# A two-layer graph kernel on one Trainium2 core: its gather ring in two pools, additions of beta pinned, ranks scattered in pairs

## The chip, the cores and the metric

The kernel runs on one core of one Trainium2 chip. A core has a matrix engine (TensorE, PE in the profile), a vector engine (VectorE, DVE), a scalar engine (ScalarE, ACT), a general engine (GpSimd, POOL) and one that only issues transfers (SyncE, SP). Each takes its own instructions in order and waits for others by semaphores. A name with a q (SPq, ACTq) is an engine's issuing side. The metric is device microseconds (us) of one execution, lower is better; three runs before the change gave a median of 2438.08.

## The reference, and what is computed

x has 8 batches of 2048 nodes with 256 features; adj is a sparse symmetric 2048x2048 matrix with a full diagonal. Two layers run one after the other, both over the same adj:

```python
# layer 0: attention, softmax within chunks of 256 columns, 4 heads
scores = clip(q @ k / 8, -10, 10); scores = where(mask == 0, -10, scores)
ctx = softmax_per_chunk(scores) @ v
out = ctx @ Wo.T + bo + x
out = (out - mean) * rsqrt(var + 1e-5) * gamma + beta
x = layernorm(x + out)
# layer 1: attention by e = s_src[j] + s_dst[i], leaky relu 0.2, masked softmax, then elu
x = layernorm(x + elu(alpha @ (x @ W)))
```

## The kernel before, in words

Everything is float32. The batches are taken in four pairs (g = 0 to 3, `G = 2`); the nodes in 16 blocks of 128 (`NT`). Since adj is sparse, each node gathers only its neighbours.

**Row lists** (`edge_lists`, lines 45 to 168). Sixteen steps load 128 rows of adj each (line 72, alternately on SP and ACT), mark the neighbours with their column number (line 74, with `jrow`, which comes from an iota on GpSimd, lines 57 to 59), count them on ACT (line 76) and take the largest 24 column numbers (lines 86 to 92). After each step one table step of pair 0 follows (`between`, line 96). Then each node gets its rank by number of neighbours: eight blocks on VectorE (line 106) and, beside them, eight on ACT (line 109), with a correction and a cast to integers for all (111, 113). GpSimd scatters the records of 16 blocks to DRAM in order of rank (line 117), SP loads them sorted (`srt`, line 120), and VectorE makes from them `node`, `nodeb`, `valid`, `idx` and the masks `same` (lines 124 to 148). After sorting, a block's row lists have a known longest length: `CAPS`, 24 slots for block 0 down to 5 for block 15, 164 in all.

**Tables** (`tables`, lines 351 to 409). For each pair and block: keys and values (`kv_d`) and queries with the residual (`qx_d`) are made on PE, copied by ACT and stored by SP. Every second step loads the next x (`load_x`, line 318) into one of two buffers `xt`, transposes it (line 334), and hands the previous `xt` to `add_beta` (line 344), which adds beta on GpSimd (line 348) and stores it (SP, line 349). The buffer is free for the next load after that store.

**Passes.** The main loop (lines 786 to 825) takes 64 steps of layer 0, order 15, 13, ... 1, 0, 2, ... 14 within a pass over one pair, and from the third pass on 32 steps of layer 1 between and after them. A step of layer 0 gathers by indirect transfer from GpSimd, a slot (one neighbour for 128 nodes) at a time (line 475, `fetch0`), multiplies with the query (VectorE, lines 533 and 540), sums by head on PE (552, 562), takes the softmax (line 573 on), weights the values (VectorE 487, ACT 493), sums them on PE (500) and copies the context out (ACT, line 612). `fetch` runs one step ahead. Pass g also makes the tables of pair g + 1, one block a step.

**Ring.** Gathered slots lie in 14 units of two slots each (`RING`, `UNIT`, lines 422 to 430), taken in turn. Each is zeroed once by VectorE, since a gather leaves slots without a neighbour as they were.

**What sets the order.** The kernel is written against a scheduler. It places the instructions of each engine by its own estimate of when they are ready, near the order of the source but not in it, and gives buffers from pools. When a pool is closed its memory goes to later pools, whose first use waits for the last use of the old tiles. So the pools of the preparation (`prep`, lines 234 to 293), of the lists (416) and of the ring (422) share memory in that order.

Of the kernel before, what the change touches and what calls it, by code (L numbers as in the profile page):

```python
# [9 lines left out]
F32 = mybir.dt.float32  # L10
BF16 = mybir.dt.bfloat16
I32 = mybir.dt.int32
I8 = mybir.dt.int8
AF = mybir.ActivationFunctionType
ALU = mybir.AluOpType
AX = mybir.AxisListType

P = 128
# [16 lines left out]
TOP = 24  # L35
REC = 32
G = 2
UNIT = 2
RING = 14
WW = 520  # L40
EMIN = 4.5399929762484854e-05

# [2 lines left out]
def edge_lists(tc: tile.TileContext, pool, bank, adj, const, ident, rec_d, B, between):  # L45
# [4 lines left out]
    nc = tc.nc  # L50
    N = adj.shape[0]
    NT = N // P
# [9 lines left out]
    rec = pool.tile([P, NT, REC], F32, name="rec")  # L62
# [5 lines left out]
    krow = pool.tile([P, N], F32, name="krow")  # L68

    for it in range(NT):  # L70
# [4 lines left out]
        junk = pool.tile([P, N], BF16, tag="junk", name="junk", bufs=1)  # L75
        nc.scalar.activation(junk, v, AF.Sign, accum_out=rec[:, it, TOP:TOP + 1])
        nc.vector.scalar_tensor_tensor(key[:, it:it + 1], rec[:, it, TOP:TOP + 1], float(N), nid[:, it:it + 1],
                                       op0=ALU.mult, op1=ALU.add)
# [9 lines left out]
        for r in range(TOP // 8):  # L88
            top = rec[:, it, r * 8:(r + 1) * 8]
            nc.vector.max(out=top, in_=cf)  # L90
            if r + 1 < TOP // 8:
# [3 lines left out]
                                accum_out=rec[:, it, TOP + 1:TOP + 2])  # L95
        between(it)


    rank = const.tile([P, NT], F32, name="rank")

    half = NT // 2
    nkey = pool.tile([P, NT], F32, name="nkey")
    nc.vector.tensor_scalar(nkey, key, -1.0, None, op0=ALU.mult)
    for it in range(half):
        gt = pool.tile([P, N], F32, tag="v", name="v", bufs=2)
        nc.vector.tensor_scalar(gt, krow, key[:, it:it + 1], 0.0, op0=ALU.is_gt, op1=ALU.add,
                                accum_out=rank[:, it:it + 1])
        junk = pool.tile([P, N], BF16, tag="junk", name="junk", bufs=1)
        nc.scalar.activation(junk, krow, AF.Sign, bias=nkey[:, half + it:half + it + 1],
                             accum_out=rank[:, half + it:half + it + 1])  # L110
    nc.vector.tensor_scalar(rank[:, half:], rank[:, half:], 0.5, 0.5 * (N - 1), op0=ALU.mult, op1=ALU.add)
    rank_i = pool.tile([P, NT], I32, name="rank_i")
    nc.vector.tensor_copy(rank_i, rank)

    views = dram_disjoint_views(rec_d, NT)
    for it in range(NT):
        nc.gpsimd.indirect_dma_start(out=views[it], out_offset=bass.IndirectOffsetOnAxis(ap=rank_i[:, it:it + 1], axis=0),
                                     in_=rec[:, it, :], in_offset=None)
    srt = pool.tile([P, NT, REC], F32, name="srt")
    nc.sync.dma_start(srt, rec_d.rearrange("(t p) r -> p t r", p=P))  # L120

    vals = srt[:, :, 0:TOP]
    node = const.tile([P, NT], I32, name="node")
    nc.vector.tensor_copy(node, srt[:, :, TOP + 2])
    nodeb = const.tile([P, NT, 2 * G], I32, name="nodeb")
    for b in range(2 * G):
        nc.vector.tensor_scalar(nodeb[:, :, b], srt[:, :, TOP + 2], float((B - 2 * G + b) * N), None, op0=ALU.add)
    valid = const.tile([P, NT, TOP], I8, name="valid")
    nc.vector.tensor_scalar(valid, vals, 0.0, None, op0=ALU.is_gt)
    far = pool.tile([P, NT, TOP], F32, name="far")  # L130
# [1 line left out]
    nc.vector.scalar_tensor_tensor(far, vals, -1.0, far, op0=ALU.add, op1=ALU.add)  # L132
    idx = const.tile([P, NT, TOP], I32, name="idx")
    nc.vector.tensor_copy(idx, far)

    chunk = pool.tile([P, NT, TOP], F32, name="chunk")
    nc.vector.tensor_scalar(chunk, vals, 0.0, None, op0=ALU.is_gt)
# [26 lines left out]
    op = bank("mf", 1)[0:1, 0:1]  # L164
# [7 lines left out]
def sparse_path(ctx: ExitStack, tc: tile.TileContext, keep, x, adj, Wq, bq, Wk, bk, Wv, bv, Wo, bo, gamma, beta, W, a,  # L172
                out):
    nc = tc.nc
    B, N, F = x.shape
    KC = F // P
    NT = N // P
# [6 lines left out]
    rec_d = nc.dram_tensor("rec_d", [N, REC], F32).ap()  # L184
# [5 lines left out]

    wh_d = [nc.dram_tensor(f"wh_d{p}", [N, 2 * WW], F32).ap() for p in range(NG // 2)]

# [4 lines left out]
    const = ctx.enter_context(tc.tile_pool(name="const", bufs=1))  # L197
# [8 lines left out]
    eps = const.tile([P, 1], F32, name="eps")  # L206
    nc.gpsimd.memset(eps, EPS)
    gamma_r = const.tile([P, F], F32, name="gamma_r")
    beta_r = const.tile([P, F], F32, name="beta_r")
# [24 lines left out]
    with tc.tile_pool(name="prep", bufs=2) as prep:  # L234
# [36 lines left out]
        for k, (v, scale) in enumerate(((bq, 0.125), (bk, 1.0))):  # L271
# [3 lines left out]
                                 scale=scale)  # L275
# [68 lines left out]
    def add_beta(g, t):  # L344

        xt = xTs.pop((g, t))[2]
        xv = xt.rearrange("p k (b f) -> p (k b) f", b=G)
        nc.gpsimd.tensor_tensor(xv, xv, beta_r.unsqueeze(1).to_broadcast([P, 2 * G, F]), op=ALU.add)  # L348
        nc.sync.dma_start(qx_d[g][t * P:(t + 2) * P, GF:].rearrange("(k p) f -> p k f", p=P), xt)

    def tables(g, t):
        if t % 2 == 0:
            if t:
                add_beta(g, t - 2)
            if g * NT + t + 2 < NG * NT:
                load_x(*divmod(g * NT + t + 2, NT))
            chunk_x(g, t)
        xT, xC, xt = xTs[g, t - t % 2]
        rows = slice(t % 2 * P, (t % 2 + 1) * P)
        if t == NT - 1:  # L360
            add_beta(g, t - 1)
# [49 lines left out]
    def first_tables(t):  # L411
        if t == 0:
            load_x(0, 0)
        tables(0, t)

    with tc.tile_pool(name="lists", bufs=1) as pool:
        with nc.allow_low_precision("exact small integers"):
            idx, valid, same, node, nodeb, rank, over = edge_lists(tc, pool, bank, adj, const, ident, rec_d, B,
                                                             first_tables)
        nc.vector.tensor_copy(keep, over)  # L420

    ring = ctx.enter_context(tc.tile_pool(name="ring", bufs=1))

    def unit():

        return ring.tile([P, UNIT, 2 * WW], F32, tag="u", name="u", bufs=RING)


    for _ in range(RING):
        nc.vector.memset(unit(), 0.0)  # L430
    sd = [const.tile([P, NT, 2, GH], F32, name=f"sd{p % 2}") for p in range(2)]

    def spread(src, sums, n):
# [35 lines left out]
    def gather(width, table, idx, t):  # L469
        units = []  # L470
        for s0 in range(0, CAPS[t], UNIT):
            u = unit()
            n = min(UNIT, CAPS[t] - s0)
            for k in range(n):
                nc.gpsimd.indirect_dma_start(  # L475
                    out=u[:, k, 0:width], out_offset=None, in_=table,
                    in_offset=bass.IndirectOffsetOnAxis(ap=idx[:, t, s0 + k:s0 + k + 1], axis=0),
                    bounds_check=N - 1, oob_is_err=False)
            units.append((u[:, 0:n], s0, n))
        return units  # L480
# [8 lines left out]
    def weighted_act(part, al, s0, n):  # L489
        for k in range(n):  # L490
            for e in range(part.shape[2] // D):
                pe = part[:, k, e * D:(e + 1) * D]
                nc.scalar.activation(pe, pe, AF.Copy, scale=al[:, e, s0 + k:s0 + k + 1])  # L493
# [23 lines left out]
    def scores0(g, t):  # L517
# [46 lines left out]
        for unit in units[npe:]:  # L564
            reduced(*unit)
# [73 lines left out]
    def rows1(g, t):  # L639
# [4 lines left out]
        nc.scalar.copy(xT, pt)  # L644
        wh = work.tile([P, WW], F32, tag="whs", name="whs")
        for b in range(G):
# [5 lines left out]
            nc.scalar.copy(wh[:, GF + b * H:GF + (b + 1) * H], pw[:, F + H:F + 2 * H])  # L652
        nc.sync.dma_start(wh_d[g // 2][t * P:(t + 1) * P, g % 2 * WW:(g % 2 + 1) * WW], wh)

# [3 lines left out]
    def fetch1(p, t):  # L658
        got1[p, t] = gather(2 * WW, wh_d[p], idx1, t)

# [28 lines left out]
    def context1(p, t):  # L689
# [5 lines left out]
        for i, (u, s0, n) in enumerate(units):  # L695
            for k in range(2):
                if i >= len(units) - na[k]:
                    weighted_act(u[:, :, k * WW:k * WW + GF], e[:, k * GH:(k + 1) * GH], s0, n)
        for i, (u, s0, n) in enumerate(units):
# [72 lines left out]
    def at(i):  # L772
        return i // NT, order[i % NT]
# [12 lines left out]
    for k, (layer, i) in enumerate(seq):  # L786
        g, t = at(i)
# [46 lines left out]
@with_exitstack  # L834
def kernel(ctx: ExitStack, tc: tile.TileContext, *args):
    nc = tc.nc
    flag = ctx.enter_context(tc.tile_pool(name="flag", bufs=1))
    over = flag.tile([1, 1], I32, name="over_keep")
    sparse_path(tc, over, *args)
    n_over = nc.values_load(over[0:1, 0:1], min_val=0, max_val=1 << 20)  # L840
    with tc.If(n_over > 0):
        dense_path(tc, *args)
# [417 lines left out]
```

## Time and profile before

| what | us |
|---|---|
| median of 3 runs (lowest, highest) | 2438.08 (2430.17, 2441.8) |
| the profiled execution | 2424.8 |
| its span on the core | 2423.1 |
| busy PE / DVE / ACT / POOL | 1885.1 / 1842.2 / 1401.9 / 1472.6 |
| copies of the context (line 612), step 0 / 15 / 16 / 31 | at 284.4 / 648.7 / 669.6 / 1033.2 |

Busy time is the sum of an engine's instructions within the span, so 1885.1 of 2423.1 means that PE was at work 78% of it, over stages with different limits. Times of instructions are counted from the start of the span. A line such as L348 is that of the kernel before, with the numbers printed above.

### The profile page before, as it was taken

What the parts mean: (1) busy time and instruction counts of PE and PEld (TensorE: products, weight loads), DVE (VectorE), ACT (ScalarE), POOL (GpSimd) and SP (SyncE); (2) the same over time, 40 slices, a digit from 0 to 9 for tenths busy, and PEclk for the clock granted to TensorE, in tenths of its full rate; (3) what the DMA queues carried; (4) which work ended last, traced back from release to release, by engine and by line L of the source; (5) the groups of instructions that cost most, each with busy time, mean ns of one, the idle gap of its engine ahead of it and who ended that gap; (6) DMA issues with size and microseconds to landing.
All of it is one profiled execution on the core that took longest, in us unless ns stands there. A gap on an engine that the chain in (4) does not pass through costs nothing. (4 is left out here: it accounts for less than half of the span.)

```text
span 2423.1 us, 38937 instructions
## 1 busy us (share of the span) xinstructions
PE 1885.1 (78%) x11946; PEld 1618.3 (67%) x11946; DVE 1842.2 (76%) x4095; ACT 1401.9 (58%) x5031; POOL 1472.6 (61%) x1225
## 2 busy tenths in 40 slices
PE   6786886689888889898899997776767775455764
PEld 5665675577777778777777776765666665445653
DVE  5975567878767888778889887887878886556775
ACT  4582354355555566555566675666346577556766
POOL 1123644686546667366678657775778754767874
PEclk9998898899989999999999998897888987777877
DMA  6745877598879679598879979896679975986873
GB/s 221 278 172 159 314 266 249 209 337 320 291 261 319 249 267 388 180 375 316 300 267 351 346 247 360 306 308 216 220 254 334 360 256 185 386 279 231 282 277 111
DMA packets 240750, 669.11 MB, mean 276 GB/s; under 512 B 44455, under 2 KB 70826, under 8 KB 238486
## 3 DMA queue, kind: packets, MB, share of 16 engines
q0 software_dynamic: 156800, 505.01, 59.1%
q1 hardware_dynamic: 80016, 151.56, 17.0%
q10 hardware_dynamic: 3718, 9.97, 1.2%
q8 instruction: 98, 1.61, 0.3%
q14 instruction: 118, 0.97, 0.1%
HBM read 612.79 MB, written 126.36 MB: 305 GB/s over the span
## 5 line engine op out<-in xcount | busy, mean ns | idle before, releaser
L475 POOL DMA_INDIRECT u<-kv_d,idx x656 | 802.2, 1223 | 423.0 <-PE acc L500 159.2
L500 PE MATMUL acc<-ident,u 128*128 128x128 f32 x5248 | 727.7, 295 | 191.6 <-DVE u L487 118.4
L500 PEld LDWEIGHTS acc<-ident,u 128*128 128x128 f32 x5248 | 649.9, 153 | 254.8 <-DVE u L487 166.1
L475 POOL DMA_INDIRECT u<-wh_d,idx x328 | 398.5, 1215 | 158.7 <-issue 68.9
L552 PE MATMUL pr<-ident,u 128*128 128x128 f32 (+1 forms) x1984 | 280.5, 291 | 78.5 <-DVE u L533 62.4
L487 DVE TENSOR_TENSOR u<-u,al 128x1024 f32<-128x1024 f32 x280 | 331.2, 1216 | 1.3
L533 DVE TENSOR_TENSOR u<-u,qx 128x1024 f32<-128x1024 f32 (+1 forms) x248 | 296.4, 1195 | 32.1 <-DMA u<-kv_d,idx 25.7
L487 DVE TENSOR_TENSOR u<-u,z 128x1024 f32<-128x1024 f32 x266 | 315.0, 1213 | 0.8
L552 PEld LDWEIGHTS pr<-ident,u 128*128 128x128 f32 (+1 forms) x1984 | 240.9, 148 | 108.0 <-DVE u L533 85.7
L493 ACT ACTIVATE u<-u,z 128x64 f32<-128x64 f32 x1008 | 261.0, 336 | 27.2 <-DVE z L686 27.2
L493 ACT ACTIVATE u<-u,al 128x64 f32<-128x64 f32 x800 | 210.7, 342 | 39.0 <-DVE al L593 38.4
L348 POOL TENSOR_TENSOR xt<-xt,beta_r 128x1024 f32<-128x1024 f32 x32 | 78.6, 2462 | 177.9 <-PE tk L334 151.6
L382 PE MATMUL tk<-wq,xT 128*128 128x256 f32 x512 | 149.6, 408 | 37.3 <-ACT kvs L376 37.3
L649 PE MATMUL mf<-wa,x1T 128*128 128x264 f32 x512 | 158.5, 435 | 21.0 <-ACT x1T L644 10.9
L369 PE MATMUL tk<-wkv,xT 128*128 128x256 f32 x512 | 144.9, 396 | 14.7 <-ACT xC L339 14.5
L621 PE MATMUL mf<-wo,cT 128*128 128x256 f32 x512 | 144.8, 406 | 10.6 <-ACT whs L652 9.9
L373 PE MATMUL tk<-wkv,xC 128*128 128x256 f32 x512 | 144.4, 398 | 0.0
L540 DVE TENSOR_TENSOR u<-u,qx 128x1024 f32<-128x1024 f32 (+1 forms) x96 | 110.3, 1152 | 44.6 <-DMA qx<-qx_d,node 23.9
L649 PEld LDWEIGHTS mf<-wa,x1T 128*128 128x128 f32 x512 | 97.4, 208 | 55.3 <-ACT whs L652 23.3
L441 ACT ACTIVATE sq<-o,nm 128x256 bf16<-128x256 f32 x256 | 129.4, 506 | 5.0
L382 PEld LDWEIGHTS tk<-wq,xT 128*128 128x128 f32 x512 | 94.4, 204 | 51.0 <-ACT kvs L376 42.0
L437 ACT ACTIVATE nm<-sums 128x2 f32<-128x2 f32 (+1 forms) x160 | 32.4, 202 | 160.0 <-DVE sums L627 82.0
(166 smaller groups left out, 3164.9 us busy)
## 6 DMA issues: line engine op xcount, KB each, us to landing
kv_d<-kvs SPq DMA_DIRECT2D x48, 512.0 KB
wh_d<-whs SPq DMA_DIRECT2D x64, 260.0 KB
xt<-in_x_dram SPq DMA_DIRECT2D x64, 256.0 KB
qx_d<-xt SPq DMA_DIRECT2D x32, 512.0 KB
qx_d<-qs SPq DMA_DIRECT2D x64, 256.0 KB
x_d<-o SPq DMA_DIRECT2D x64, 256.0 KB
xr<-x_d SPq DMA_DIRECT2D x32, 512.0 KB
u<-kv_d,idx POOLq DMA_INDIRECT x656, 6.5
```

Source lines behind the costliest of these rows:

```text
L369: nc.tensor.matmul(pm[:, 0:F], xT[:, b * KC + kc, rows], wkv[:, kc, 0:F], start=(kc == 0), stop=False, skip_group_check=True)
L373: nc.tensor.matmul(pm[:, F:], xC[:, b * KC + kc, rows], wkv[:, kc, F:], start=False, stop=(kc == KC - 1), skip_group_check=True)
L382: nc.tensor.matmul(qb, xT[:, b * KC + kc, rows], wq[:, kc, :], start=(b == 0 and kc == 0), stop=False, skip_group_check=True)
L441: nc.scalar.activation(sq, src[:, k, :], AF.Square, bias=nm[:, k:k + 1], accum_out=m2[:, k:k + 1])
L475: nc.gpsimd.indirect_dma_start(out=u[:, k, 0:width], out_offset=None, in_=table, in_offset=bass.IndirectOffsetOnAxis(ap=idx[:, t, s0 + k:s ...
L487: nc.vector.tensor_tensor(pv, pv, av, op=ALU.mult)
L493: nc.scalar.activation(pe, pe, AF.Copy, scale=al[:, e, s0 + k:s0 + k + 1])
L500: nc.tensor.matmul(acc[:, c, :], part[:, k, c * P:(c + 1) * P], ident, is_transpose=True, start=first and k == 0 and c == 0, stop=last and ...
L533: nc.vector.tensor_tensor(prod.rearrange("p k j (s w) -> p k j s w", w=W8), u[:, :, 0:GF].rearrange("p s (k j w) -> p k j s w", k=UNIT, w=W8),
L552: nc.tensor.matmul(pr[0:n * W8, k, :], prod[:, j // (NJ // UNIT), j % (NJ // UNIT), :], ident, is_transpose=True, start=(j == 0), stop=(j ...
L621: nc.tensor.matmul(po[:, b, :], cT[:, b * KC + kc, :], wo[:, kc, :], start=(b == 0 and kc == 0), stop=False, skip_group_check=True)
L649: nc.tensor.matmul(pw[:, 0:F + 2 * H], xT[:, b * KC + kc, :], wa[:, kc, :], start=(kc == 0), stop=(kc == KC - 1))
```

## The change

Five edits, all but one in the part before the first gather:

- The ring has two pools. `ring0` has five units (`RING0`) and is opened ahead of the lists' pool, so that it takes memory beside the lists; `ring1` has nine and is opened after it. Units are still taken in turn, 14 in all.
- The five units of `ring0` are zeroed by GpSimd ahead of the lists; of the nine of `ring1`, five are zeroed by ACT (a copy with scale 0) and four by VectorE.
- The addition of beta is held in the order of the source (`keep_in_program_order`) for all 32 of its calls.
- Ranks are corrected and cast pair by pair, block `it` with block 8 + `it`, and each pair of blocks is scattered at once; before, all sixteen followed the last rank.
- `nodeb`, which only the last scatters use, stands after `idx` in the source.

```diff
+RING0 = 5
@@ edge_lists
+    views = dram_disjoint_views(rec_d, NT)
     for it in range(half):
         gt = pool.tile([P, N], F32, tag="v", name="v", bufs=2)
         nc.vector.tensor_scalar(gt, krow, key[:, it:it + 1], 0.0, op0=ALU.is_gt, op1=ALU.add,
                                 accum_out=rank[:, it:it + 1])
         junk = pool.tile([P, N], BF16, tag="junk", name="junk", bufs=1)
-        nc.scalar.activation(junk, krow, AF.Sign, bias=nkey[:, half + it:half + it + 1],
-                             accum_out=rank[:, half + it:half + it + 1])
-    nc.vector.tensor_scalar(rank[:, half:], rank[:, half:], 0.5, 0.5 * (N - 1), op0=ALU.mult, op1=ALU.add)
-    rank_i = pool.tile([P, NT], I32, name="rank_i")
-    nc.vector.tensor_copy(rank_i, rank)
-
-    views = dram_disjoint_views(rec_d, NT)
-    for it in range(NT):
-        nc.gpsimd.indirect_dma_start(out=views[it], out_offset=bass.IndirectOffsetOnAxis(ap=rank_i[:, it:it + 1], axis=0),
-                                     in_=rec[:, it, :], in_offset=None)
+        k = half + it
+        nc.scalar.activation(junk, krow, AF.Sign, bias=nkey[:, k:k + 1], accum_out=rank[:, k:k + 1])
+        nc.vector.tensor_scalar(rank[:, k:k + 1], rank[:, k:k + 1], 0.5, 0.5 * (N - 1), op0=ALU.mult, op1=ALU.add)
+        nc.vector.tensor_copy(rank_i.rearrange("p (h t) -> p t h", h=2)[:, it], rank.rearrange("p (h t) -> p t h", h=2)[:, it])
+        for k in (it, half + it):
+            nc.gpsimd.indirect_dma_start(out=views[k],
+                                         out_offset=bass.IndirectOffsetOnAxis(ap=rank_i[:, k:k + 1], axis=0),
+                                         in_=rec[:, k, :], in_offset=None)
...
-    nodeb = const.tile([P, NT, 2 * G], I32, name="nodeb")
-    for b in range(2 * G):
-        nc.vector.tensor_scalar(nodeb[:, :, b], srt[:, :, TOP + 2], float((B - 2 * G + b) * N), None, op0=ALU.add)
...
     nc.vector.tensor_copy(idx, far)
+    nodeb = const.tile([P, NT, 2 * G], I32, name="nodeb")
+    for b in range(2 * G):
+        nc.vector.tensor_scalar(nodeb[:, :, b], srt[:, :, TOP + 2], float((B - 2 * G + b) * N), None, op0=ALU.add)
@@ add_beta
-        nc.gpsimd.tensor_tensor(xv, xv, beta_r.unsqueeze(1).to_broadcast([P, 2 * G, F]), op=ALU.add)
+        tc.keep_in_program_order(
+            nc.gpsimd.tensor_tensor(xv, xv, beta_r.unsqueeze(1).to_broadcast([P, 2 * G, F]), op=ALU.add))
@@ ahead of the lists' pool
+    rings, turn = [ctx.enter_context(tc.tile_pool(name="ring0", bufs=1))], [0]
+
+    def unit():
+
+        k = int(turn[0] % RING >= RING0)
+        turn[0] += 1
+        return rings[k].tile([P, UNIT, 2 * WW], F32, tag="u", name="u", bufs=RING - RING0 if k else RING0)
+
+    for _ in range(RING0):
+        nc.gpsimd.memset(unit(), 0.0)
+
@@ after it
-    ring = ctx.enter_context(tc.tile_pool(name="ring", bufs=1))
-
-    def unit():
-
-        return ring.tile([P, UNIT, 2 * WW], F32, tag="u", name="u", bufs=RING)
-
-    for _ in range(RING):
-        nc.vector.memset(unit(), 0.0)
+    rings.append(ctx.enter_context(tc.tile_pool(name="ring1", bufs=1)))
+    for n in range(RING0, RING):
+        u = unit().rearrange("p s w -> p (s w)")
+        if n % 2:
+            nc.scalar.activation(u, eps.to_broadcast([P, UNIT * 2 * WW]), AF.Copy, scale=0.0)
+        else:
+            nc.vector.memset(u, 0.0)
```

More of the change, by code (lines that the diff above doesn't have):

```diff
@@ L99, in edge_lists @@
     rank = const.tile([P, NT], F32, name="rank")
+    rank_i = pool.tile([P, NT], I32, name="rank_i")
     half = NT // 2
```

## The prediction, made before the changed kernel had run

> **What bounds the kernel now.** I read the totals first, then the busy time by stage, then GpSimd's, VectorE's and SyncE's instructions in order of time around the weakest stage. The stages (columns: window, its length, busy time and instruction count of PE, its weight loads, DVE, ACT, POOL, then granted TensorE clock, DMA share, GB/s):
>
> ```profile
> 0.00:160.00 160.00, 121.16 (x564) 97.09 (x564) 123.23 (x447) 92.22 (x211) 24.42 (x56) 0.93 0.66 233
> 160.00:200.00 40.00, 26.61 (x144) 22.05 (x144) 7.80 (x11) 19.41 (x53) 20.21 (x18) 0.93 0.35 112
> 200.00:280.00 80.00, 57.77 (x265) 46.52 (x266) 46.47 (x73) 25.91 (x94) 33.71 (x28) 0.82 0.70 239
> 280.00:650.00 370.00, 309.04 (x1980) 265.61 (x1979) 287.81 (x564) 186.05 (x696) 228.15 (x187) 0.92 0.81 285
> 650.00:1040.00 390.00, 347.83 (x2240) 298.08 (x2239) 300.07 (x618) 227.44 (x890) 225.38 (x179) 0.96 0.78 279
> ```
>
> From 650 on PE is busy 89% (347.8 of 390) and sets the pace with DVE. From 160 to 280 nothing is near full: PE 84.4 of 120 us, DVE 54.3, POOL 53.9. That is the gap between the row lists and the first gathers, and nearly all of the change lies there. GpSimd in order of time (start, duration, what, in brackets idle before and releaser):
>
> ```profile
> 17.86 2.48 POOL L348 TENSOR_TENSOR xt<-xt,beta_r 128x1024 f32<-128x1024 f32 x1 [15.41 <-DMA beta_r<-in_L_gnn_beta_dram]
> 24.61 1.83 POOL L57 IOTA v<- 128x2048 int32 x1 [4.27 <-PE mf L291]
> ...
> 173.01 1.13 POOL L117 DMA_INDIRECT rec_d<-rec,rank_i  x1 [8.62 <-ACT kvs L376]
> ...
> 200.76 3.42 POOL L513 DMA_INDIRECT qx<-qx_d,node  x1 [5.31 <-DVE node L124]
> ...
> 249.47 2.35 POOL L348 TENSOR_TENSOR xt<-xt,beta_r 128x1024 f32<-128x1024 f32 x1 [17.93 <-PE tk L334]
> 251.97 1.02 POOL L475 DMA_INDIRECT u<-kv_d,idx  x1
> ```
>
> The first gather stands behind three additions of beta (210.3, 229.2, 249.5) that wait for transposes of tables needed only a pass later. VectorE says what else was late:
>
> ```profile
> 32.04 4.49 DVE L74 SCALAR_TENSOR_TENSOR v<-at,jrow 128x2048 f32<-128x2048 int32 x2 [3.13 <-DMA at<-in_adj_dram]
> ...
> 200.31 0.17 DVE L124 CAST node<-srt 128x16 int32<-128x16 f32 x1 [28.17 <-DMA srt<-rec_d]
> ...
> 202.47 0.35 DVE L134 CAST idx<-far 128x384 int32<-128x384 f32 x1
> ...
> 213.66 1.79 DVE L430 MEMSET u<- 128x2080 f32 x1 [0.56 <-issue]
> ...
> 258.94 1.23 DVE L540 TENSOR_TENSOR u<-u,qx 128x1024 f32<-128x1024 f32 x1 [15.22 <-DMA u<-kv_d,idx]
> ```
>
> The row lists' indices exist at 202.8, the first zeroed unit at 215.5, the first gather goes at 252.0. SyncE holds one more delay: the sorted records (srt) were loaded only after the store of another addition, done at 195.45:
>
> ```profile
> 195.47 0.37 SPq L349 DMA_DIRECT2D qx_d<-xt  x1
> 196.13 0.37 SPq L120 DMA_DIRECT2D srt<-rec_d  x1
> ```
>
> [...] 0.82 granted where PE is busy 72% (200 to 280), 0.96 at 89% (650 to 1040); so matmuls moved out of the gap get no dearer. [...] one addition of 4.21 us against a median 2.357 looks like it, so GpSimd's memsets may cost double, in time that GpSimd has to spare.
>
> **The change part by part** (times of the new kernel are estimates on its own clock).
>
> *Start.* Before, the pools' memory made the iota and the adjacency loads wait for the preparation's last read (PE L291, 24.6 us). In the new instruction order that wait is on the five ring memsets instead; the iota stands ahead of every addition, the first adjacency load stands on ACT's queue behind Wo's (issued at 12.5 before), the second on SP behind the first addition's store. beta_r is issued about 3 us earlier, so that store goes at about 17.5 instead of 20.4. Second tile landed at about 22, its 2.25 us operation done by 24.8, where before it was 36.5: 11.7 us earlier. Not all of it lasts: ACT must copy 12 tables before the first rank activation in both orders, and tables came every 9.7 us (36.85 to 143.58 for twelve). These start some 6 us earlier. I take 9, ends 6 and 12.
>
> *Ranks in pairs.* Before: last rank at 171.7, sixteen scatters of 1.26 us pitch (20 us) from 173.0, then SP's store, load at 196.13, landed 200.31. After: ACT's pace (8 activations in 24 us, 3.0 each) covers a pair of scatters (2.5); the 14 extra small DVE operations (0.17 each, 2.4 us) lie in DVE's wait for ACT, since its own eight passes take 18.2. Past the last rank stand 0.5 (correction, cast), 0.4 (issue), 2.5 (pair) and the write's landing[...]. The load on SP now stands behind the last table's kv store, no addition. 171.7 - 9 + 5.4 = 168.1, plus the old 4.2 to land: 172.3 against 200.3. One addition stands between the scatters; its transposes came at 162.0 before, inside the rank stage, so 0 (ends 0 and 3).
>
> *Row lists first.* In the built order all four nodeb operations still precede idx, so 0; idx at 174.8.
>
> *Ring and pins.* One qx gather (3.4 and 0.3), then gathers from 178.5, against 252.0; none of the additions of the second pass stands ahead of the first 29. Five units hold the first nine gathers (11.7 us), by when ring1 is being zeroed. First product: gathered data took 7.0 us (252.0 to 258.9), so 185.5; VectorE's lists take 12.8 after the load and end at 185.1. Then VectorE's four memsets (2.17 pitch, 8.7 us; fourteen took 30.4 before) and ACT's five zeroings beside them. An activation of 128x2048 took 1.91 here; five make 9.7 us, over by 195, while ACT's next need is the product's copy at about 201. GpSimd's five memsets: 512 elements took 0.52, so 2.1 to 4 each, 10 to 20 us, before the second addition. From 195.4 the chain reduce, products, scores, softmax, sum took 24 us before (260.2 to 284.4), some 6 of it waits for gathers: the first context is copied at about 213, against 284.4. Gain there 71.
>
> *What is late next.* ACT's order has 18 tables ahead of that copy, where before had 24; six tables of 7.3 us of PE (read at full clock, 24.4 to 31.7) move into the first pass, 44 us. Are they paid? Before, that pass ran fifteen steps from 284.4 to 648.7 (364.3 us) with 9 tables; the second pass, same row lists, ran them from 669.6 to 1033.2 (363.6 us) with 15. The first pass has 61 us of idle PE and clock 0.92, so the new pass with 14 tables should take what the second takes: 364, to 577 against 648.7. From there the orders are near alike (GpSimd's last 606 instructions the same), so I add 1 us for the pins. Sum: -70. The profiled execution took 2424.8 (span 2423.1); that gives 2355. The median of the runs is 13.3 above it; carried over, 2438.1 - 70 = 2368.
>
> **Rivals.**
> 1. *PE takes it back.* If the first pass is bound by PE as the second is at 89%, the moved 44 us return: gain 27, 2411. For it: after 280 DVE's longest wait in total is on PE (tf L562, 109.9 us). Against: second pass equally long with more tables. 0.13.
> 2. *The zeroing keeps its place.* ACT or ring1 late, gathers beyond the ninth stalling until lists, memsets and tables are through, or the adjacency start lost: gain 45, 2393. 0.12.
> 3. *More.* Clock 0.96 instead of 0.92 over 309 us of PE saves 13, and without the stall from 340 to 380 (PE 30.5 of 40) some more: gain 88, 2350. 0.15.
> 4. *Slower: pinned additions starve PE.* Every later addition now stands behind gathers that wait for ring slots; its store and the next x load follow it on SP, and PE transposes that x in a fixed place. Before, none of these waited after 250 (the nine waits on PE, 151.6 us in all, are earlier). About 24 pins remain; it decides from 3 us of PE stall each (24 x 3 = 72), and at 5 each costs 120: 2488. Against: the new order places each transposition about two steps (some 45 us) behind its addition, while addition, store and load need about 12. 0.05.
>
> **How the numbers follow.** Forecast 0.53 (2352 to 2385), rivals 0.13, 0.12, 0.15, 0.05, no visible change 0.02. The range must leave out no more than 2 in 10: 2338 takes in case 3, 2404 takes in case 2 and the start's lower end; left out are most of case 1, case 4 and tails. A measurement tells 0.5% from no change, 12 us (before's runs spread over 11.6). Faster 0.93, same 0.02, slower 0.05.
>
> **What would show it.** Second adjacency product ended near 25; sorted records used near 172; first gather near 179; first context copy near 213; sixteenth near 577 and PE above 88% between them. Wrong if the first pass is much longer than 364 (rival 1 or 4: waits of PE's L334 transposes for x loads tell 4), or if gathers stall between the ninth and tenth (rival 2).

## The result, and the profile after

| | us |
|---|---|
| median after (4 runs) | 2405.7 (2400.65 to 2415.02) |
| median before, same chip (4 runs) | 2439.9 |
| ratio | 0.9874, interval 0.9838 to 0.9910 |
| span of the profiled execution | 2398.9 (before 2423.1) |

The change gains 34 us where 70 were forecast. The landmarks that the prediction named, beside the trace (the last column is the best kernel of the experiments below):

| event, us from the start | before | forecast | after | best |
|---|---|---|---|---|
| second adjacency product ends | 36.5 | 24.8 | 28.1 | |
| first rank pass on VectorE starts | 149.1 | 140 | 148.5 | |
| sorted records used | 200.3 | 172.3 | 191.0 | 180.4 |
| first gather | 252.0 | 178.5 | 195.5 | |
| first context copied | 284.4 | 213 | 246.2 | 225.4 |
| sixteenth | 648.7 | 577 | 617.0 | 579.3 |
| 48th | 1455.7 | | 1437.7 | 1390.2 |
| 64th | 1983.3 | | 1963.1 | 1906.8 |

Lines in the changed kernel are shifted: L348 (addition) is now L351, L349 (its store) L352, L334 (transposes of x) L336, L475 (gather) L489, L364 (rank copy into `kvs`) L367, L375 and L376 (copies into `kvs`) L378 and L379, L377 (kv store) L380, L120 (load of the sorted records) L122, L558 (`prT`) L572, L612 (context) L626.

The stages after, in the columns of the prediction's first fence:

```profile
160.00:200.00 40.00, 25.63 (x107) 20.56 (x106) 14.76 (x39) 18.81 (x50) 20.73 (x20) 0.76 0.39 125
200.00:280.00 80.00, 55.72 (x287) 45.37 (x286) 49.12 (x94) 32.13 (x89) 44.47 (x41) 0.82 0.86 292
280.00:650.00 370.00, 328.91 (x2084) 282.32 (x2083) 275.98 (x543) 200.52 (x756) 216.61 (x172) 0.93 0.79 277
650.00:1040.00 390.00, 357.07 (x2332) 304.83 (x2330) 317.42 (x632) 232.44 (x911) 252.34 (x196) 0.98 0.85 305
```

The gap from 160 to 280 is still there: PE is busy 81.4 of 120 us, before 84.4. The work that follows has moved forward, but the gap has not filled. What stands in it shows in three queues between the last rank and the first context. GpSimd (start, duration, what, in brackets idle before and releaser):

```profile
173.80 0.97 POOL L118 DMA_INDIRECT rec_d<-rec,rank_i  x1 [0.30 <-issue]
174.79 2.35 POOL L351 TENSOR_TENSOR xt<-xt,beta_r 128x1024 f32<-128x1024 f32 x1
177.30 0.98 POOL L118 DMA_INDIRECT rec_d<-rec,rank_i  x1 [0.17 <-DVE rank_i L116]
...
183.68 0.97 POOL L118 DMA_INDIRECT rec_d<-rec,rank_i  x1 [0.30 <-issue]
193.96 1.25 POOL L527 DMA_INDIRECT qx<-qx_d,node  x1 [9.31 <-DVE neg L687]
```

SyncE, whose queue holds the rest behind the addition's store:

```profile
177.16 0.37 SPq L352 DMA_DIRECT2D qx_d<-xt  x1
179.99 0.90 SPq L320 DMA_DIRECT2D xt<-in_x_dram  x2
180.98 0.42 SPq L380 DMA_DIRECT2D kv_d<-kvs  x1
181.50 0.38 SPq L391 DMA_DIRECT2D qx_d<-qs  x1
186.25 0.32 SPq L380 DMA_DIRECT2D kv_d<-kvs  x1
186.88 0.37 SPq L122 DMA_DIRECT2D srt<-rec_d  x1
```

And ScalarE, which writes every table into one `kvs` buffer:

```profile
170.03 0.39 ACT L379 COPY kvs<-tk 128x256 f32<-128x256 f32 x1
...
185.02 0.37 ACT L378 COPY kvs<-tk 128x256 f32<-128x256 f32 x1 [11.09 <-DMA kv_d<-kvs]
...
229.40 0.19 ACT L367 COPY kvs<-rank 128x1 f32<-128x1 f32 x1 [4.81 <-DMA kv_d<-kvs]
229.50 0.26 ACT L572 COPY prT<-pr 128x128 f32<-128x128 f32 x1
...
245.66 0.19 ACT L367 COPY kvs<-rank 128x1 f32<-128x1 f32 x1 [8.19 <-DMA kv_d<-kvs]
245.75 0.36 ACT L572 COPY prT<-pr 128x256 f32<-128x256 f32 x1
246.02 0.26 ACT L574 COPY prT<-pr 64x128 f32<-64x128 f32 x1
246.18 0.58 ACT L626 COPY cT<-acc 128x512 f32<-128x512 f32 x1
```

Read them together. Table 14 lay finished in `kvs` at 170.4, but its store was queued on SyncE behind the store of an addition that GpSimd began only at 174.79, between scatters. It was issued at 180.98, so ScalarE could write the last table at 185.02, that one was stored at 186.25, and only then did SyncE issue the load of the sorted records. The scatters themselves were hardly earlier. Six of them stood behind the addition; the last was issued at 183.68, and its landing came 2.4 us after that in the trace, at about 186.1. The table's store therefore ended the wait of the load, but by only half a us: two chains, both with this addition in them, came to their end together. Later a copy of one column of ranks waits 4.81 and 8.19 us for the same buffer, each time straight ahead of copies that the first steps need.

### The profile page after: what moved, and what is told of

It reads as the page before. It is cut to its first block, busy times and chain, and to the rows that moved or that the text cites. A ratio compares the mean times of both kernels' runs of the same rounds, so it can differ in the third digit from the quotient of the medians.

```text
span 2398.9 us, 38927 instructions
## 1 busy us (share of the span) xinstructions
PE 1872.2 (78%) x11946; PEld 1599.8 (67%) x11946; DVE 1838.5 (77%) x4099; ACT 1407.8 (59%) x5036; POOL 1497.8 (62%) x1230
## 5 line engine op out<-in xcount | busy, mean ns | idle before, releaser
L489 POOL DMA_INDIRECT u<-kv_d,idx x656 | 811.7, 1237 | 421.5 <-PE acc L514 155.9
L514 PE MATMUL acc<-ident,u 128*128 128x128 f32 x5248 | 719.2, 292 | 197.0 <-DVE u L501 126.5
L514 PEld LDWEIGHTS acc<-ident,u 128*128 128x128 f32 x5248 | 641.8, 152 | 260.7 <-DVE u L501 172.0
L489 POOL DMA_INDIRECT u<-wh_d,idx x328 | 403.4, 1230 | 155.0 <-issue 67.1
L547 DVE TENSOR_TENSOR u<-u,qx 128x1024 f32<-128x1024 f32 (+1 forms) x248 | 299.6, 1208 | 26.3 <-DMA u<-kv_d,idx 23.6
L663 PE MATMUL mf<-wa,x1T 128*128 128x264 f32 x512 | 158.9, 436 | 18.5 <-ACT x1T L658 10.2
L351 POOL TENSOR_TENSOR xt<-xt,beta_r 128x1024 f32<-128x1024 f32 x32 | 78.2, 2445 | 141.1 <-PE tk L336 99.8
L385 PE MATMUL tk<-wq,xT 128*128 128x256 f32 x512 | 143.4, 393 | 23.6 <-ACT kvs L379 23.6
L372 PE MATMUL tk<-wkv,xT 128*128 128x256 f32 x512 | 150.4, 408 | 13.6 <-ACT xC L341 13.2
L376 PE MATMUL tk<-wkv,xC 128*128 128x256 f32 x512 | 145.4, 399 | 0.0
L635 PE MATMUL mf<-wo,cT 128*128 128x256 f32 x512 | 139.0, 394 | 3.9 <-ACT whs L666 2.7
L554 DVE TENSOR_TENSOR u<-u,qx 128x1024 f32<-128x1024 f32 (+1 forms) x96 | 114.7, 1200 | 13.4 <-DMA qx<-qx_d,node 6.7
L590 DVE TENSOR_SCALAR sc<-tf 128x64 f32<-128x64 f32 (+5 forms) x64 | 14.0, 218 | 135.1 <-PE tf L576 135.1
```

The lines of the kernel that those rows point to most:

```text
L372: nc.tensor.matmul(pm[:, 0:F], xT[:, b * KC + kc, rows], wkv[:, kc, 0:F], start=(kc == 0), stop=False, skip_group_check=True)
L376: nc.tensor.matmul(pm[:, F:], xC[:, b * KC + kc, rows], wkv[:, kc, F:], start=False, stop=(kc == KC - 1), skip_group_check=True)
L385: nc.tensor.matmul(qb, xT[:, b * KC + kc, rows], wq[:, kc, :], start=(b == 0 and kc == 0), stop=False, skip_group_check=True)
L489: nc.gpsimd.indirect_dma_start(out=u[:, k, 0:width], out_offset=None, in_=table, in_offset=bass.IndirectOffsetOnAxis(ap=idx[:, t, s0 + k:s ...
L514: nc.tensor.matmul(acc[:, c, :], part[:, k, c * P:(c + 1) * P], ident, is_transpose=True, start=first and k == 0 and c == 0, stop=last and ...
L547: nc.vector.tensor_tensor(prod.rearrange("p k j (s w) -> p k j s w", w=W8), u[:, :, 0:GF].rearrange("p s (k j w) -> p k j s w", k=UNIT, w=W8),
```

## The experiments

Sixteen runs. The kernel before had 2436.3 (first group), 2434.9 (second) and 2433.5 (fourth), so these groups can be set side by side. On the chip of the third group the kernel before took 2666.4, at a granted TensorE clock of 0.848 to 0.863 where the other groups have 0.885 to 0.897; times of that group are compared only with one another, and its traces are used up to the first context. Landmarks come from one profiled execution of each kernel, times from medians.

### Which edits carry the gain

**No pins.** `tc.keep_in_program_order(...)` around the addition taken away, the rest kept.

> The changed kernel with its additions of beta left to the scheduler; ring, pairs and lists as changed. In the built order only one addition comes ahead of the first gathers, and the rest of GpSimd's order is nearly as with the pins. Theory A (the gain is the earlier first context, its shortfall lies in queues that stand behind single buffers): within 6 us of the changed kernel's 2405.7, first context within 5 us of 246. Theory B (the pinned additions make PE wait for x, 30 us in the changed kernel): 2375 to 2390, and those waits gone.

2378.9, ratio 0.9783 (0.9743 to 0.9823): the pins cost 27 us, the time of theory B. The wait that it rested on is not gone, only elsewhere: PE now waits 15.8 us for x in the first pass (1.2 in the changed kernel), where it costs nothing that shows (first context 243.2, sixteenth 618.0). But from 1040 to 1480 these waits fall from 13.6 us to 1.5.

**One ring, as before.** Pins and pairs kept.

> The changed kernel with the ring of before: one pool after the lists, fourteen memsets on VectorE; pins and pairs kept. Theory A: the first gathers wait for the first memsets behind the lists, the first product for all fourteen; first context some 20 us later than 246, time 2420 to 2432. Theory C (PE takes moved work back, so that a later start with 22 tables ahead instead of 18 costs little): 2403 to 2412.

2442.1, ratio 1.0026 (0.9995 to 1.0057). More than either theory had: without the two pools nothing is left, so the ring is worth 36 us. Not all of that is the zeroing. The adjacency products began at 32.1 again, as before (32.0; 20.1 in the changed kernel), and the first rank pass only at 159.0. VectorE zeroed all fourteen units until 247.4, and the first context came at 273.7.

**Scatters all after the last rank, as before.**

> The changed kernel with ranks corrected, cast and scattered as before, after the last rank. My prediction gave the pairs 17 us; theory A, from the trace, gives them 0 to 8, because the last six scatters of the pairs end at 184.6 against 193.1 before: sorted records landed at 191 to 197, time 2403 to 2415. If the pairs are worth what was predicted: 2420 or more.

2411.0, ratio 0.9888 (0.9841 to 0.9935), 5 us above the changed kernel, and the intervals overlap. The sorted records were used at 197.6 instead of 191.0: pairs bring 6.6 us, not the 19 that the working of that step gives beside its 9 for the start. Yet the first context came 4 us sooner here (242.1), and the sixteenth 7 us later (624.1): sorted records and first context need not move together.

**`ring1` zeroed by VectorE alone.**

> The changed kernel with the nine units of the second pool zeroed by VectorE alone, ACT's five zeroings gone (VectorE gets five more memsets of 2.17 us pitch, 10.9 us). Theory A: ACT is free for the tables' copies, but the first product's reduction comes 11 us later; first context 243 to 258, time 2403 to 2418. If ACT's zeroing is what delays the first context (the 9.6 us before PE's transposes at 220.4): first context 236 to 242, time 2395 to 2402.

2422.0, ratio 0.9950 (0.9932 to 0.9968), 16 us above and later than either theory: the five zeroings on ScalarE earn their place, though in the changed kernel GpSimd's tenth gather waits 5.39 us for the first of them. How they earn it is open. The first context came 20 us later (266.4), but the sixteenth at 617.4, as in the changed kernel (617.0); PE had been at other work, 60.5 us of the 80 from 200 to 280 instead of 55.7. The loss comes after that (15.6 us at the 41st context), and no run says why.

**Pins on the additions of pair 1 alone.**

```diff
-        tc.keep_in_program_order(nc.gpsimd.tensor_tensor(xv, ...))
+        add = nc.gpsimd.tensor_tensor(xv, ...)
+        if g == 1:
+            tc.keep_in_program_order(add)
```

> The changed kernel with the pin on the additions of pair 1 alone; those of pairs 2 and 3 are free again, and with that the 22nd, 28th and 29th addition on GpSimd stand after 268, 437 and 437 gathers instead of 315, 440 and 472. Theory A (the pins cost because these late additions hold SP's x loads, and PE then waits for x, 9.3 us near 1297): 2374 to 2388, first context still near 246, those waits of PE gone. Theory B (the cost lies in the pins of pair 1, the 9th and 14th addition, in the first pass): 2398 to 2412.

2380.0 (its profiled execution, 2393, was the longest of four), ratio 0.9767 (0.9715 to 0.9820): theory A. PE's waits for x from 1040 to 1480 fall to 0.6 us. The run frees the additions of pair 0 as well, but up to the sixteenth context (615.3 instead of 617.0) that changed next to nothing. So what the pins cost comes from the additions of pairs 2 and 3. The place shows in the changed kernel, on GpSimd, SyncE, PE and GpSimd again:

```profile
1275.55 2.36 POOL L351 TENSOR_TENSOR xt<-xt,beta_r 128x1024 f32<-128x1024 f32 x1
1282.82 0.63 SPq L352 DMA_DIRECT2D qx_d<-xt  x1
1288.99 1.08 SPq L320 DMA_DIRECT2D xt<-in_x_dram  x2
1296.91 0.48 PE L336 MATMUL tk<-ident,xt 128*128 128x128 f32 x1 [6.62 <-DMA xt<-in_x_dram]
1300.05 0.90 PE L336 MATMUL tk<-ident,xt 128*128 128x128 f32 x3 [2.66 <-DMA xt<-in_x_dram]
1420.28 1.20 POOL L489 DMA_INDIRECT u<-kv_d,idx  x1 [23.22 <-DVE r L462]
```

With no pins the same addition runs 76 us sooner, and PE doesn't wait:

```profile
1199.09 2.35 POOL L350 TENSOR_TENSOR xt<-xt,beta_r 128x1024 f32<-128x1024 f32 x1
```

The pinned addition waits behind 35 more gathers (472 instead of 437), its store and the x load follow, and PE stands 9.3 us, a third of the cost. The addition before it (1220.9 instead of 1194.1) is followed by 2.5 us more. Then GpSimd stands 23.2 us where, with no pins, its longest wait was 9.64. From 1320 to 1450 (changed kernel, then no pins) GpSimd is busy 78 us instead of 93 and DMA 0.81 instead of 0.92:

```profile
1320.00:1450.00 130.00, 114.08 (x749) 98.37 (x748) 110.94 (x251) 83.47 (x311) 78.25 (x63) 0.94 0.81 291
```

```profile
1320.00:1450.00 130.00, 113.98 (x737) 98.48 (x736) 109.70 (x256) 84.80 (x315) 92.60 (x73) 0.91 0.92 337
```

From 1450 to 1520 both run DMA at 0.92 to 0.93, so gathers that were not made by then are not caught up: the 44th context is 17 us later than with no pins, the 55th 30. That the rest of the loss is carried by these gathers is read from the trace; no run takes it apart.

### Does PE take the earlier start back?

**Less PE in the first pass.** `add_bias` left out in the tables of pair 1.

> The changed kernel without the 128 bias transposes on PE (the biases of k and q) in the tables of pair 1, so the output leaves these out. Each was 0.27 us of PE in the first pass, with their weight loads some 27 us in all. Theory A (PE bounds the first pass): sixteenth context 588 to 600 instead of 617, first context as before within 8 us, time 2375 to 2390. Theory B (the pass is held by gathers, ring or the chain through ACT): sixteenth context 610 or later, time 2398 to 2410.

2443.6, ratio 1.0033 (1.0016 to 1.0051), sixteenth context 632.2. PE had 340.4 us of work from 200 to 617 instead of 356.4, and the pass took longer: 388.6 instead of 370.8. Theory A is not borne out, but it isn't refuted either: the scheduler also moved other instructions in this kernel, and PE waited 36.7 us for x between 200 and 1480 (15.1 in the changed kernel). The run shows only that less work on PE did not by itself shorten the pass.

**Rank column by one transfer.** The copy of a rank column into `kvs` before each table of pair 1 is replaced:

```diff
-        if g == PG:
-            nc.scalar.copy(kvs[:, 2 * GF:], rank[:, t:t + 1])
...
+    nc.sync.dma_start(kv_d[PG].rearrange("(t p) c -> p t c", p=P)[:, :, 2 * GF:], rank.unsqueeze(2))
```

> The changed kernel with the rank column of pair 1's table written by one transfer from SP, in place of sixteen copies on ScalarE into the only kvs buffer, each of which waits for the store before (67.6 us in 15 waits, 4.8 and 8.2 of them straight ahead of the first context). Theory A (these waits are what the first context lost, and what is won there stays): first context 230 to 237, sixteenth 600 to 608, time 2386 to 2398. Theory B (the first pass is set by PE from 200 on, so an earlier first context is taken back): first context 230 to 240, sixteenth 613 to 620, time 2400 to 2410.

2383.4, ratio 0.9783 (0.9729 to 0.9837): theory A, with 22 us a little more than it had. ScalarE's longest waits from 160 to 620, changed kernel first (engine, line, what it waited for, us in total, times, longest):

```profile
ACT kvs L367 <- DMA kv_d<-kvs: 67.6, 15, 8.2
ACT nm L451 <- DVE o L647: 18.5, 10, 3.2
```

```profile
ACT nm L450 <- DVE sums L640: 25.1, 12, 3.9
ACT kvs L376 <- DMA kv_d<-kvs: 22.2, 4, 11.1
```

Sixteen copies of 0.19 us cost the pass 17 us: it runs 354.0 instead of 370.8 (and 357.0 and 352.3 in the two kernels below that leave them out as well). They stand ahead of `prT` in ScalarE's order, and in the changed kernel fifteen of them hold ScalarE until the last table's store is through. The first context gains only 6.5 us (239.7; 230 to 237 was expected), since part of the wait passes to the copies of the table itself.

**Both: no pins and the rank column by one transfer.**

> The rank column by one transfer and no pins. If the two costs are apart and add up: 2360 to 2370 by theory A of the rank column, 2374 to 2386 by its theory B. If the gain of the free additions was an accident of one instruction order, it goes here: 2390 to 2410.

2361.8, ratio 0.9706 (0.9652 to 0.9760), and again in the fourth group:

> No pins and the rank column by one transfer, beside the changed kernel: 40 to 48 us below it if the two gains hold (26 and 22 apart), under 30 if they were accidents of one measurement.

2358.1 beside 2410.7 of the changed kernel run again (below): 52.6 us, more than the 40 to 48 expected. With 43.9 us in the group before, the two costs (27 and 22 apart) add up, and neither is an accident of one order.

### What held the start

**The scatter path.** Corrections and casts on GpSimd ahead of their scatters, and the one addition on VectorE:

```diff
-        nc.vector.tensor_scalar(rank[:, k:k + 1], ...)
-        nc.vector.tensor_copy(rank_i...)
+        nc.gpsimd.tensor_scalar(rank[:, k:k + 1], ...)
+        nc.gpsimd.tensor_copy(rank_i...)
@@ add_beta
+        eng = nc.vector if (g, t) == (0, NT - 2) else nc.gpsimd
```

> The changed kernel with the rank corrections and casts on GpSimd, right ahead of their scatters, and the addition of block pair 14 of pair 0, which stood between the scatters (174.79), on VectorE. The order on PE, ScalarE and SP stays as it was. Theory A (this addition held SP's store, behind it the kv store of table 14 and the load of the sorted records, and VectorE's late casts held the scatters): last scatter ends near 178 instead of 184.6, kv store of table 14 near 171 instead of 181, sorted records used at 181 to 186 instead of 191.0, first context 236 to 241 instead of 246.2, time 2393 to 2401. Theory B (the last table's copies set it whatever the scatters do): sorted records used at 188 or later, time within 4 us of 2406.

Sorted records used at 182.5 and first context at 238.9, as theory A has it. Whether that reaches the end, the fourth group tells. In it the changed kernel ran again as the mark:

> The changed kernel itself, as the mark for the three beside it on the same chip: ratio to before 0.984 to 0.991, 2398 to 2412 if before is near 2437.

2410.7, ratio 0.9895 (0.9857 to 0.9933). Beside it:

> The scatter path alone (casts on GpSimd, one addition on VectorE), beside the changed kernel. Theory A (the 7 to 8 us by which its first context is sooner stay to the end): 6 to 12 us below the changed kernel. Theory B (the first pass takes them back, because tables on PE and ScalarE set its length): within 4 us of it.

2388.1, ratio 0.9827 (0.9785 to 0.9869), 22.6 us below the mark; the two intervals still overlap by 0.001. SyncE there, then in the mark:

```profile
167.75 0.37 SPq L353 DMA_DIRECT2D qx_d<-xt  x1
...
171.55 0.42 SPq L381 DMA_DIRECT2D kv_d<-kvs  x1
...
176.97 0.32 SPq L381 DMA_DIRECT2D kv_d<-kvs  x1
179.93 0.37 SPq L122 DMA_DIRECT2D srt<-rec_d  x1
```

```profile
181.71 0.42 SPq L380 DMA_DIRECT2D kv_d<-kvs  x1
...
187.62 0.37 SPq L122 DMA_DIRECT2D srt<-rec_d  x1
```

The kv store of table 14 goes 10.2 us sooner, the load of the sorted records 7.7. The edit moves both chains that ended at this load: the addition's store, and the scatters, the last of which now goes out at 176.36 instead of 184.42. In this trace the load waits 2.3 us for the scatters and no longer for a store. What each chain is worth alone, no run tells; from the landing at 186.1 above, freeing the store alone would have won the load about half a us. First context 232.0 against 244.5, sixteenth 601.0 against 613.2: 12 us won and kept. By the 41st context it is 14.5, by the 64th 21, more than either theory had; no run explains this rest.

**Two `kvs` buffers**, for one `qx` buffer less.

> The changed kernel with two kvs buffers instead of one, paid for with one qx buffer less (three instead of four). Theory A (the one kvs buffer sets the pace of the tables in the list stage, 9.7 us each, and with it the start of the rank pass): first rank pass at 138 to 143 instead of 148.5, first context 232 to 240, time 2375 to 2397. Theory B (PE and ScalarE set that pace): first rank pass at 147 to 149, time 2400 or more, since a query gather then waits sooner for its buffer.

The rank pass on VectorE:

```profile
140.96 2.35 DVE L110 TENSOR_SCALAR_CACHE_REDUCE v<-krow,key 128x2048 f32<-128x2048 f32 x1 [4.68 <-ACT krow L84]
```

in place of, in the changed kernel:

```profile
148.53 2.35 DVE L110 TENSOR_SCALAR_CACHE_REDUCE v<-krow,key 128x2048 f32<-128x2048 f32 x1 [8.00 <-ACT krow L84]
```

Theory A for the start: ScalarE's waits for kv stores in the list stage (15.1 us in four) are gone and the ranks begin where the forecast had them. The time is no gain, though: 2638.5 (ratio 0.9946, 0.9914 to 0.9978), beside 2599.9 (0.9804) of the scatter path on the same chip. The changed kernel did not run there; elsewhere it had 0.9874 and 0.9895. Put together with no pins, rank transfer and scatter path:

> The same with two kvs buffers and three qx buffers. Theory A of the two buffers: 2335 to 2352. Theory B: 2355 to 2375.

2607.4 (ratio 0.9833) beside 2573.2 (0.9719) of the same kernel with one `kvs` and four `qx` on that chip. So the start was not worth a `qx` buffer in either pair; whether the missing buffer or the other order that comes with it costs more than the start brings isn't shown.

### The best version

**No pins, rank column by one transfer, scatter path.** On the chip of the third group:

> No pins, the rank column by one transfer, and the scatter path of the first run of this group. If the 8 us of the scatter path are apart from the others: 2350 to 2358. If the first pass takes them back: 2359 to 2366.

Ratio 0.9719 (0.9652 to 0.9786) there, too wide to tell. In the fourth group:

> The same with the scatter path. Theory A: 6 to 12 us below the kernel with no pins and the rank column by one transfer. Theory B: within 4 us of it.

2346.3, ratio 0.9641 (0.9599 to 0.9684), 64 us below the changed kernel and 11.8 below the same kernel without the scatter path (0.9704, 0.9657 to 0.9751, so the intervals overlap a little), as its theory A had it. Its gap:

```profile
200.00:280.00 80.00, 71.06 (x453) 59.96 (x452) 63.04 (x118) 47.17 (x149) 57.77 (x48) 0.94 0.92 332
```

PE 71.1 of 80 us at clock 0.94, where the changed kernel had 55.7 at 0.82. Its sixteenth context comes at 579.3; the forecast for the change was 577.

## Why the prediction was wrong

The direction and the part that carries the gain, the ring, were right. The size was not: 2368 against 2405.7, just past the upper end of the range (2404). What failed, step by step:

- **Start, 9 us:** 0.6. The products did come sooner (28.1, 8.4 us; 11.7 forecast), and VectorE was through its lists at 140.5 instead of 149.1, but then waited 8.00 us for `krow` on ScalarE, behind the twelfth table. ScalarE copied `krow` at 147.85, before at 146.90: its tables had not moved at all. The prediction named this floor and took for granted that the tables would start some 6 us earlier. Their pace was set by the one `kvs` buffer, as two buffers show (140.96).
- **Ranks in pairs, sorted records at 172.3:** 191.0, 18.7 late, in two parts. ScalarE's last rank was done at 173.9 where the working has 162.7 (171.7 less 9): 11.2, which is the lost start and a slower rank stage on ScalarE. From there to the use of the records it took 17.1 us instead of 9.6: 7.5. The failing sentence of this step is "One addition stands between the scatters; its transposes came at 162.0 before, inside the rank stage, so 0 (ends 0 and 3)". Its operands were ready, its place was not: in GpSimd's fixed order it stood behind ten scatters and ahead of six, VectorE's casts for four of the pairs came in one group at 167, and its store stood on SyncE ahead of the kv store and with that ahead of the load of the sorted records. The prediction said that the load would stand behind the last table's kv store, "no addition", but not what that store stands behind. With the scatter path the 17.1 us are 11.0, and 12 us are won at the first context and at the sixteenth.
- **Row lists first, 0:** right. The first gather follows the sorted records by 4.5 us (6.2 forecast).
- **First context at 213:** 33 us late. 18.7 come with the sorted records. From the first gather to the first product it took 11.3 us instead of 7.0, and from the last memset (over at 216.8) to the context 29.4 us where the prediction took 24 less 6. ScalarE's rank copies and zeroings stand in that chain: a copy waits until 209.96, and only behind it do the five zeroings run, until 220.1, where the prediction had them over by 195. It did not look at what else ScalarE had queued.
- **First pass 364 us with 14 tables:** 370.8. It was taken from the second pass, whose tables have no rank column. With the rank copies gone the pass takes 354. So the estimate was near by luck; ScalarE had waited for these copies in the kernel before too, 53.5 us in eleven waits.
- **Pins, +1 us:** 27. The mis-sized term behind it is rival 4, which named the mechanism, place and sign (PE's transposes waiting for x loads behind late additions), and priced it at about 24 pins of 3 to 5 us each or nothing. It is two additions in the third pass, 12 us of PE waits, and gathers that are then missing.
- **PE takes it back (rival 1):** not in that way. PE is at 89% from 280 to 650 (328.9 of 370), as "above 88%" asked, and yet the rank transfer shortens the pass by 17 us with no PE work removed. A share of 89% didn't mean that PE set the time. But a later start can be made up: with the zeroing on VectorE alone, 20 us lost at the first context were gone by the sixteenth. Carrying a gain at the first context through to the end, 71 to 70 us, was itself an assumption.

For the sixteenth context the experiments nearly close the account: 613.2 for the changed kernel run again, less 12 for the scatter path, less 20 for the rank copies (613.2 to 593.7 and 593.0), give 581, and 579.3 was measured. To the end it does not close. The changed kernel was 40 us behind the forecast at the sixteenth context, and the pins cost 27 more, but the gain fell short by only 36. With no pins the lead over the kernel before is 31 us at the sixteenth context and still 31 at the 48th, then 48 at the 55th. The prediction took this lead as constant; no run explains the growth. It hid a part of the miss, and that was luck.

## What to carry to other kernels

Follow a moved instruction through every queue it feeds, not just its own: here one addition of 2.35 us held six scatters in its own queue, and beside them an SP store, behind it a table's store and a single buffer on ScalarE, and the load at the end waited for both. A cheap copy into a single buffer costs what the buffer's last store still needs, and a program order that puts it ahead of work on the path makes everything wait. A pin is priced where its instruction lands later than it would freely, by what follows it downstream; compare the two orders place by place instead of multiplying a price by the number of pins. And an earlier first output is not yet a gain: two of the runs above moved the first context one way and the sixteenth another, or not at all.

## What the runs showed that was not expected

- VectorE's last cast in the changed kernel, two elements per partition, took 3.02 us instead of 0.17, and ended at 177.17, just after the addition on GpSimd (174.79 to 177.14):

```profile
170.10 0.17 DVE L116 CAST rank_i<-rank 128x2 int32<-128x2 f32 x1
173.97 0.15 DVE L115 TENSOR_SCALAR rank<-rank 128x1 f32<-128x1 f32 x1 [3.69 <-ACT junk L114]
174.15 3.02 DVE L116 CAST rank_i<-rank 128x2 int32<-128x2 f32 x1
```

  Why it took that long, no run shows. And it held nothing up. In the changed kernel run again the same cast took 0.17 us, over before the addition began:

```profile
173.29 0.17 DVE L116 CAST rank_i<-rank 128x2 int32<-128x2 f32 x1
```

  There the addition began at 175.52, the first scatter behind it at 178.03 and the load of the sorted records at 187.62, each 0.7 us later than in the first trace.
- GpSimd's five zeroings of the ring took 8.92 us together (27.93 to 36.85 in the changed kernel), 1.8 each, where the prediction allowed 2.1 to 4: none of them took double.
- The landing of the scatters' writes, a term of the prediction's 5.4 us past the last rank that was not read from a trace, is in the traces after all: 2.1 us from issue to landing in the kernel before, 2.1 to 3.1 in the changed one. With the scatter path the load was issued 3.6 us after the last scatter's issue began (176.36 to 179.93).
- Leaving 128 PE instructions out made the kernel 38 us slower than the changed one (2443.6), a warning against reading a small difference between two instruction orders as the cost of the edited part.
